# Row sums of adj by transpose and VectorE, first transfers in another order, a full tile for leftover taps, distances two groups at a time

## The chip, the core and the metric

One Trainium2 chip runs the program on one of its cores. A core has TensorE (PE; its weight loads are listed apart as PEld), VectorE (DVE), ScalarE (ACT), GpSimd (POOL) and SyncE (SP). Each engine works through its own queue in order; between engines there are semaphores. SP here only issues DMAs; ACT and POOL issue a few as well. The metric is the device time of one execution in microseconds, as a median of several runs, beside one execution taken by the profiler. Everything is float32.

## What is computed

Two graph layers over 128 graphs of 128 nodes with 256 features, `adj` sparse with about 3% of its entries set. Cut to what matters:

```python
# layer 0
in_degrees = jnp.sum(adj, axis=-1)
norm = jnp.power(in_degrees + 1e-06, -0.5)[..., None]
f_hom = jnp.einsum('bnd,de->bne', x, theta) * norm
f_hom = jnp.einsum('bnm,bmd->bnd', adj, f_hom) * norm
f_het = jnp.einsum('bnd,de->bne', x, W_h)
gate = sigmoid(x @ W_t + b_t)
x = layernorm(x + elu(gate * f_hom + (1 - gate) * f_het))
# layer 1
h = relu(bn1(conv1(xc)))            # xc: x with nodes along the last axis
h = bn2(conv2(h))                   # 17 taps along the nodes
x_conv = relu(h + xc)
s = x @ w_se.T + b_se               # three coordinates a node
dist = sq_n + sq_m - 2 s_n . s_m
A = jnp.exp(-dist) * adj
x_nmp = A @ relu(x @ w_msg.T + b_msg)
gi, gh = [x_conv, x_nmp] @ w_ih.T + b_ih, x @ w_hh.T + b_hh
x = layernorm(x + gru_update(gi, gh, x))
```

The degree of a node, the sum over a row of `adj`, scales both sides of layer 0's aggregation. The kernel receives `adj` turned, as `adjT[m, b, n]`, because a matmul's stationary operand is wanted with the summed axis on the partitions.

## The kernel before

The work has three stages.

**Layer 0 and the way into the convolution (0 to about 735 us).** A loop over rounds `t` from -1 to 63 (L511) takes two graphs a round (J = 2) and is pipelined by hand: in round t the projections of pair t (`l0_project`, L317 and L322) run beside the end of pair t-1 and the turning and first convolution of pair t-2. At the end of a round, `l0_turn(t+1)` (L291) transposes the next x by TensorE (L284), copies it from PSUM on VectorE (L288), and makes the degrees: for each graph one matmul with `adjT` stationary and a single column of ones streamed (L297). VectorE copies two columns out (L301), and POOL raises them to -1/2 (L161, L162; `inv_sqrt`). ScalarE uses the result as `norm` when it reads the next round's projection (L326). Then `l0_mix(t)` (L343) aggregates with `adjT` and VectorE reads that (L348).

In the same rounds TensorE also turns the taps of the 17-tap convolution into 136 frequency weights, written to memory as `w_d`. 32 units `w_unit` handle the first 128 frequencies from four row strips of 17 taps (L423). 19 units `v_unit` handle the 8 leftover ones (L455): two sets of seven input features by 17 taps, 119 rows, are multiplied by a block table `TL` of 56 columns. `TL` is filled by 14 small DMAs of POOL from the cosine table `T` (L247, in `way_back`, round 1). `units` and `units_v` put at most one such unit into a round. Taps come by `w_load` (L127, four DMAs each) into three tiles and by `v_load` (L447, two DMAs) into two rotating buffers. Before the loop SP issues `load(0)`, a weight, conv1's weights, `load(1)`, `w_load(0)` and `w_load(1)`; the other x and adjT follow from inside the rounds.

The order is written by hand for TensorE in all rounds, and for SP, VectorE and ScalarE from round 3 on (`manual_schedule`, L512). POOL's order, and that of the others in rounds -1 to 2, is found by the scheduler.

**The frequency products (735 to 912 us)** read `w_d`, multiply (L708, L721) and write `y_d`. The diff has nothing in them.

**Layer 1 (912 us to the end).** A loop over 32 groups of four graphs (G = 4; L1019), with only TensorE's order by hand. For a group: `l1_own` takes, on VectorE, a group's rows out of a turned table of coordinates (`turned`, made anew for every fourth group by two transposes, L860); `l1_kernel` makes the four distance tables by matmuls on 32-row strips (L880) into `acc`, a PSUM buffer of four banks of which there is one, which `l1_synth` (L808, L815, once in two groups) uses too; ScalarE takes the exponential (L884) and VectorE multiplies with adj (L887) into `AT`. `l1_gather` (L897) aggregates the messages with `AT`. `l1_gru` makes seven products a half group (`product`, L964), and calls `l1_kernel` of the next group between them, ahead of the fifth product of the second half.

Of the kernel before, what the change touches and what calls it, by code (L numbers as in the profile page):

```python
# [14 lines left out]
P = 128  # L15
# [19 lines left out]
def gnn_layers_kernel(ctx: ExitStack, tc: tile.TileContext, a: dict, out: bass.AP):  # L35
# [52 lines left out]
    SL = const.tile([P, P], F32, tag="SL", name="SL")  # L88
    T = taps.tile([P, M], F32, tag="T", name="T")
    FS = P // TAPS  # L90
    TL = taps.tile([P, ML * FS], F32, tag="TL", name="TL")
    conv1_w = acon.tile([P, NC, D + CO], F32, tag="conv1_w", name="conv1_w")
    shift1 = acon.tile([P, D], F32, tag="shift1", name="shift1")
    NW = 3
    wt = [taps.tile([P, 2, D], F32, tag=f"wt{i}", name=f"wt{i}") for i in range(NW)]


# [15 lines left out]
    def load(p):  # L113
        s = st[p] = {}
        s["x"] = io.tile([P, J, D], F32, tag="x", name=f"x_{p}")
        nc.sync.dma_start(s["x"], x[p * J : (p + 1) * J].rearrange("b n d -> n b d"))
        s["adjT"] = io.tile([P, J, P], F32, tag="adjT", name=f"adjT_{p}")
        nc.sync.dma_start(s["adjT"], adjT[:, p * J : (p + 1) * J, :])
# [27 lines left out]
    for i, q in enumerate("vmgb"):  # L146
        for k in range(2):
# [2 lines left out]
                vec[r : r + NC], a[f"L1_gnn_bn{k + 1}_{q}"].rearrange("(c p) -> c p", p=P)  # L150
            )

    nc.sync.dma_start(conv1_w[:, :, 0:D], a["conv1_wT"].rearrange("(c p) e -> p c e", p=P))
    nc.sync.dma_start(conv1_w[:, :, D:], a["w_seT"].rearrange("(c p) e -> p c e", p=P))
    load(1)
    w_load(0)
    w_load(1)

    def inv_sqrt(dst, src, eps, width):

# [74 lines left out]
    def way_back():  # L235

        AL = setup.tile([P, P // ML, ML], F32, tag="AL", name="AL")
        nc.vector.tensor_copy(AL, A[:, P:M].unsqueeze(1).to_broadcast([P, P // ML, ML]))
        nc.vector.memset(TL, 0.0)
        back = setup.tile([P, 1], F32, tag="back", name="back")  # L240
        nc.vector.memset(back, 2.0 / L)
        nc.vector.memset(back[0:2], 1.0 / L)

        cols = TL.rearrange("p (r i k) -> p r i k", r=2, i=FS)
        for i in range(FS):
            for r in range(2):
                nc.gpsimd.dma_start(  # L247
                    cols[i * TAPS : (i + 1) * TAPS, r, i, :], T[0:TAPS, P + r : M : 2]
                )
        tS = bank("S_ps")  # L250
        nc.tensor.transpose(tS[:, 0:P], A[:, 0:P], ident)
        nc.tensor.transpose(tS[:, P : 2 * P], AL.rearrange("p a b -> p (a b)"), ident)
        nc.vector.tensor_scalar(S, tS[:, 0:P], back, None, ALU.mult)
        nc.vector.tensor_scalar(SL, tS[:, P : 2 * P], 2.0 / L, None, ALU.mult)
# [21 lines left out]
    def nodes(q):  # L276
        return slice(q * P, (q + 1) * P)
# [13 lines left out]
    def l0_turn(p):  # L291
        s = st[p]
        s["xT"] = wf.tile([P, NC, J * P], F32, tag="xT", name=f"xT_{p}")
        transposed(s["x"], s["xT"], f"xT_{p}")
        deg = bank(f"deg_{p}")
        for j in range(J):
            nc.tensor.matmul(  # L297
                deg[:, j : j + 1], lhsT=s["adjT"][:, j, :], rhs=ones[:, 0:1], start=True, stop=True
            )
        norm = s["norm"] = small.tile([P, J], F32, tag="norm", name=f"norm_{p}")  # L300
        nc.vector.tensor_copy(norm, deg[:, 0:J])  # L301
        inv_sqrt(norm, norm, DEG_EPS, J)


# [137 lines left out]
        return [(f, min(FS, D - f)) for f in range(2 * FS * v, min(2 * FS * (v + 1), D), FS)]  # L442

    def v_load(v):
        t = taps.tile([P, 2, D], F32, tag="vt", bufs=2, name=f"v_t_{v}")
        for i, (f, n) in enumerate(v_sets(v)):
            nc.sync.dma_start(  # L447
                t[0 : n * TAPS, i, :], a["conv2_wT"][f : f + n].rearrange("i t o -> (i t) o")
            )
        s_v[v] = t  # L450

    def v_unit(v):
        n, sets = v_sets(v)[-1][1] * TAPS, len(v_sets(v))
        pl = bank(f"wl_ps_{v}")
        nc.tensor.matmul(  # L455
            pl[0 : ML * FS, 0 : sets * D], lhsT=TL[0:n],
            rhs=s_v[v][0:n, 0:sets].rearrange("p i o -> p (i o)"), start=True, stop=True,
        )
        ol = s_v[v] = taps.tile([ML * FS, 2, D], F32, tag="wl", name=f"wl_o_{v}")
        nc.vector.tensor_copy(  # L460
            ol[:, 0:sets].rearrange("p i o -> p (i o)"), pl[0 : ML * FS, 0 : sets * D]
        )
# [48 lines left out]
    for t in range(-1, NP):  # L511
        with tc.manual_schedule(engines={E.PE, E.SP, E.DVE, E.Activation} if t > 2 else {E.PE}):  # L512

            def on(q, work):
                if 0 <= q < NP:
                    work(q)

            def between():
                on(t - 1, l0_gate)
                on(t - 3, l1_analyse)  # L520

            def beside():
                on(t - 1, l0_elu)

            on(t - 2, l1_turn)
            l0_project(t, between, beside) if t >= 0 else between()
            on(t - 1, l0_norm)
            if t == 0:
                norms = batch_norms()
                next(norms)  # L530
                table(A, node, "A")
                table(T, lag, "T")

                cos, sin = T[:, 2:M:2], T[:, 3:M:2]
                both = setup.tile([P, M // 2 - 1], F32, tag="both", name="both")
                nc.vector.tensor_sub(both, sin, cos)
                nc.vector.scalar_tensor_tensor(sin, sin, -1.0, cos, ALU.mult, ALU.subtract)
                nc.vector.tensor_copy(cos, both)
            on(t - 2, l1_front)
            on(t - 2, l1_store)  # L540
            if t + 2 < NP:
                if 2 <= t + 2:
                    load(t + 2)
            else:
                m_load(t + 2 - NP)
            if t - 1 in units:
                w_store(units[t - 1])
            if t - 1 in units_v:
                v_store(units_v[t - 1])
            on(t + 1, l0_turn)  # L550
            if t == 2:
                v_load(0)
            if t == 3:
                nc.scalar.dma_start(w_msg, a["w_msgT"].rearrange("(c p) e -> p c e", p=P))
                nc.scalar.dma_start(b_msg, a["L1_gnn_b_msg"].partition_broadcast(P))
            if t == 1:
                next(norms, None)
                way_back()
                sctx.close()
                hpool = hstack.enter_context(tc.tile_pool(name="hpool", bufs=1))  # L560
                H = hpool.tile([P, NC, M, NB], F32, tag="H", name="H")
            on(t, l0_mix)
            if t in units_v:
                if units_v[t] + 1 < NV:
                    v_load(units_v[t] + 1)
                v_unit(units_v[t])
            if t in units:
                if units[t] + 2 < NU:
                    w_load(units[t] + 2)
                if t + 1 < NP:  # L570
                    w_unit(units[t])
# [299 lines left out]
        )  # L871
        st[g].update(turned=turned, own=own)

    def l1_kernel(g):
        s = st[g]
        turned, own = s["turned"], s["own"]
        pd = acc.tile([P, G, 512], F32, tag="acc", name=f"dist_ps_{g}")
        for q in range(G):
            k = slice(q * P // G, (q + 1) * P // G)
            nc.tensor.matmul(  # L880
                pd[:, q, 0:P], lhsT=turned[k, 0, :], rhs=own[k, :], start=True, stop=True
            )
        AT = ck.tile([P, G * P], F32, tag="AT", name=f"AT_{g}")
        nc.scalar.activation(  # L884
            AT.rearrange("p (q n) -> p q n", q=G), pd[:, :, 0:P], AF.Exp, scale=-1.0
        )
        nc.vector.tensor_mul(AT, AT, s["adjT"].rearrange("p q n -> p (q n)"))  # L887
        s["AT"] = AT


    def l1_gather(g):
# [115 lines left out]
    with tc.manual_schedule(engines={mybir.EngineType.PE}):  # L1007
        load_c(0)
        load_c(1)
        load_y(0)  # L1010
        for g in range(2):
            load_x1(g)
            l1_own(g)
        l1_project(0)
        l1_kernel(0)
        l1_project(1)
        l1_factors()
        l1_synth(0)
        for g in range(NG):  # L1019
            d = g // 2  # L1020
            if g + 2 < NG:
                load_c(g + 2)
                if g % 2 == 0:
                    load_y(d + 1)
                load_x1(g + 2)
            l1_gather(g)
            if 2 <= g + 1 < NG:
                l1_own(g + 1)
                l1_project(g + 1)
            l1_gru(g, 0)  # L1030
            if g % 2 == 1 and d + 1 < ND:
                l1_synth(d + 1)
            if g + 1 < NG:
                l1_gru(g, 1, {4: lambda: l1_kernel(g + 1)})
    with tc.manual_schedule(engines={E.PE, E.DVE, E.Activation}):
        l1_gru(NG - 1, 1)
    cctx.close()
# [41 lines left out]
```

## Time and profile before

| what | value |
|---|---|
| median of three runs | 2053.21 us (2051.23 to 2053.49) |
| the profiled execution | 2053.39 us, of which 2051.60 us from the first to the last instruction |
| granted TensorE clock, mean | 0.995 |
| DMA, read and written | 136.33 MB and 104.86 MB |

By stage, busy microseconds of each engine in the profiled execution:

| stretch, us | PE | DVE | ACT | POOL | granted clock | DMA share |
|---|---|---|---|---|---|---|
| 0 to 20.9 | 16.46 | 14.48 | 4.03 | 8.77 | 1.00 | 0.47 |
| 20.9 to 34.8 | 5.46 | 4.82 | 2.57 | 13.57 | 0.74 | 0.71 |
| 34.8 to 41.1 | 6.28 | 3.70 | 1.71 | 0.18 | 0.50 | 0.44 |
| 41.1 to 712 | 670.90 | 505.85 | 392.75 | 108.31 | 1.00 | 0.45 |
| 712 to 735 | 21.64 | 14.77 | 13.51 | 1.77 | 1.00 | 0.53 |
| 735 to 912 | 175.82 | 86.80 | 26.46 | 95.66 | 1.00 | 0.94 |
| 912 to 2051 | 1127.32 | 801.72 | 305.35 | 423.75 | 1.00 | 0.22 |

An engine's share of a stretch tells how full it is, not whether it sets the end; for that one looks at what each wait ended on. A float32 matmul is two records in this profile, a transpose is one; [...]the distance from one start to the next tells what one costs.

### The profile page before, as it was taken

To read this page: it belongs to the slowest core of one execution; us is meant where nothing else is said; L and a number is where in the kernel's file an instruction comes from. 1 tells how busy PE (TensorE), PEld (TensorE's weight loads), DVE (VectorE), ACT (ScalarE), POOL (GpSimd) and SP (SyncE) were. 2 spreads that over 40 slices of the span, in tenths; PEclk is the share of its full clock that TensorE was granted. 3 is DMA by queue.
4 is the path that set the end of the run, shared out by engine and by line. 5 is a ranking of instruction groups with operands and counts; after the bars stand their busy time and mean duration, and the time that the engine had idled before them with its cause. 6 is when DMAs were issued, how large, how long until landed. Compare 5 with 4: busy or idle time off the path is not lost.

```text
span 2051.6 us, 27050 instructions
## 1 busy us (share of the span) xinstructions
PE 2023.9 (99%) x8807; PEld 1384.2 (67%) x8807; DVE 1432.1 (70%) x2882; ACT 746.4 (36%) x1488; POOL 652.0 (32%) x869
## 2 busy tenths in 40 slices
PE   7999999999999999999999999999999999999997
PEld 4666766766766788886666666666666666666664
DVE  5777777777777764456767677676667767776766
ACT  2555655655555621112222222222322222232222
POOL 4111111111111135553433334333424333342431
PEclk8999999999999999999999999999999999999999
DMA  4544444444444479994222122222212222121100
GB/s 96 170 153 149 142 154 150 141 156 152 141 153 146 133 269 359 313 306 147 72 74 79 52 66 81 63 66 64 79 61 70 73 67 63 58 79 52 42 26 21
DMA packets 198044, 243.04 MB, mean 118 GB/s; under 512 B 16768, under 2 KB 141456, under 8 KB 197904
## 3 DMA queue, kind: packets, MB, share of 16 engines
q1 hardware_dynamic: 190880, 235.47, 35.3%
q10 hardware_dynamic: 6352, 5.78, 0.9%
q0 software_dynamic: 672, 0.06, 0.4%
q8 instruction: 71, 1.16, 0.3%
q14 instruction: 69, 0.57, 0.1%
HBM read 136.33 MB, written 104.86 MB: 118 GB/s over the span
## 4 chain that ended last, share of the span: by engine, by line
PE 96%; DVE 2%; POOL 1%; DMA 1%; ACT 0%; issue 0%; POOLq 0%; DVEq 0%; ACTq 0%; SPq 0%
PE g_ps L964 42%; PE f_ps L317 11%; PE conv_ps L387 5%; PE gate_ps L322 5%; PE msg_ps L844 5%; PE y_ps L708 5%; PE mix_ps L343 3%; PE coef_ps L407 3%; PE nmp_ps L897 3%; PE conv_ps L808 3%; PE z_ps L721 3%; PE x1T_ps L284 2%; PE w_ps L423 2%; PE xT_ps L284 1%; PE deg L297 1%; PE wl_ps L455 1%
## 5 line engine op out<-in xcount | busy, mean ns | idle before, releaser
L317 PE MATMUL f_ps<-w,xT 128*128 128x512 f32 x512 | 244.4, 600 | 0.1
L923 ACT ACTIVATE o<-o 128x1024 f32<-128x1024 f32 (+1 forms) x65 | 67.8, 1044 | 326.8 <-DVE o L1000 269.7
L161 POOL TENSOR_SCALAR rstd_b<-mv_b 128x2 f32<-128x2 f32 (+1 forms) x65 | 18.2, 280 | 529.6 <-DVE mv_b L262 529.6
L964 PE MATMUL g_ps<-t_h,sh 128*128 128x384 f32 x384 | 158.4, 494 | 0.0
L964 PE MATMUL g_ps<-t_c,sc 128*128 128x384 f32 x384 | 155.2, 486 | 0.0
L964 PE MATMUL g_ps<-t_m,sm 128*128 128x384 f32 x384 | 155.2, 486 | 0.0
L161 POOL TENSOR_SCALAR rstd_a<-mv_a 128x2 f32<-128x2 f32 x64 | 12.3, 193 | 436.4 <-DVE mv_a L262 380.1
L322 PEld LDWEIGHTS gate_ps<-w,xT 128*128 128x128 f32 x512 | 98.3, 192 | 69.1 <-issue 61.8
L322 PE MATMUL gate_ps<-w,xT 128*128 128x256 f32 x512 | 132.6, 382 | 0.0
L997 POOL TENSOR_TENSOR u<-u,p 128x512 f32<-128x512 f32 x63 | 79.8, 1267 | 163.3 <-DVE p L981 163.3
L317 PEld LDWEIGHTS f_ps<-w,xT 128*128 128x128 f32 x512 | 89.0, 193 | 62.9 <-issue 62.3
L708 PE MATMUL y_ps<-wb,H 128*128 128x256 f32 x544 | 128.5, 379 | 0.9 <-ACT H L411 0.8
L326 ACT ACTIVATE hom<-f_ps,norm 128x256 f32<-128x256 f32 x128 | 60.7, 474 | 187.6 <-PE f_ps L317 182.3
L271 ACT ACTIVATE y<-y,nb_b,rstd_b 128x256 f32<-128x256 f32 x128 | 70.0, 593 | 157.8 <-DVE nb_b L269 157.8
L387 PE MATMUL conv_ps<-conv_w,x1T 128*128 128x259 f32 x512 | 122.5, 381 | 0.0
L716 POOL TENSOR_TENSOR ws<-wb 128x512 f32<-128x512 f32 x67 | 93.2, 1390 | 88.8 <-PE z_ps L721 53.5
L708 PEld LDWEIGHTS y_ps<-wb,H 128*128 128x128 f32 x544 | 103.2, 190 | 15.4 <-issue 1.4
L844 PE MATMUL msg_ps<-w_msg,cx1T 128*128 128x256 f32 x480 | 108.7, 379 | 0.0
L964 PEld LDWEIGHTS g_ps<-t_c,sc 128*128 128x128 f32 x384 | 73.0, 190 | 50.9
L964 PEld LDWEIGHTS g_ps<-t_m,sm 128*128 128x128 f32 x384 | 73.0, 190 | 50.9 <-DVE sm L912 0.2
L387 PEld LDWEIGHTS conv_ps<-conv_w,x1T 128*128 128x128 f32 x512 | 97.1, 190 | 14.7 <-ACT w_o L427 0.2
L964 PE MATMUL g_ps<-w_hhT_w,cx1T 128*128 128x384 f32 x256 | 105.0, 492 | 0.0
(228 smaller groups left out, 4524.8 us busy)
## 6 DMA issues: line engine op xcount, KB each, us to landing
wb<-w_d SPq DMA_DIRECT2D x68, 512.0 KB
w_d<-w_o SPq DMA_DIRECT2D x256, 128.0 KB
y_d<-yb SPq DMA_DIRECT2D x68, 256.0 KB
x<-in_x SPq DMA_DIRECT2D x64, 256.0 KB
cx1T<-x1T_d SPq DMA_DIRECT2D x64, 256.0 KB
yt<-y_d SPq DMA_DIRECT2D x32, 512.0 KB
cx<-x_d SPq DMA_DIRECT2D x32, 512.0 KB
x_d<-x SPq DMA_DIRECT2D x63, 256.0 KB
```

The costliest lines, as they stand in the source:

```text
L271: nc.scalar.activation(dst[:, q, :], src[:, q, :], AF.Identity, bias=nb[:, q : q + 1], scale=rstd[:, q : q + 1],)
L284: nc.tensor.transpose(t[:, (c * J + j) * P : (c * J + j + 1) * P], src[:, j, c * P : (c + 1) * P], ident,)
L317: nc.tensor.matmul(pf, lhsT=xT[:, c, nodes(j)], rhs=w0[:, c, 0 : 2 * D], start=(c == 0), stop=(c == NC - 1),)
L322: nc.tensor.matmul(pg[:, j * D : (j + 1) * D], lhsT=xT[:, c, nodes(j)], rhs=w0[:, c, 2 * D : 3 * D], start=(c == 0), stop=(c == NC - 1),)
L343: nc.tensor.matmul(pm[:, j * D : (j + 1) * D], lhsT=adjT_[:, j, :], rhs=hom[:, j, :], start=True, stop=True,)
L387: nc.tensor.matmul(ph[:, 0 : D + CO], lhsT=s["x1T"][:, c, nodes(j)], rhs=conv1_w[:, c, :], start=(c == 0), stop=(c == NC - 1),)
L708: nc.tensor.matmul(py[:, blk, :], lhsT=coefs(blk if k == 0 else 2 * k + 1 - blk, c), rhs=w[:, c, blk, :], start=(c == 0), stop=(c == NC - 1),)
L716: nc.gpsimd.tensor_tensor(ws, w[:, :, 0, :], w[:, :, 1, :], ALU.add)
L844: nc.tensor.matmul(pm[:, j * D : (j + 1) * D], lhsT=x1T[:, c, nodes(q)], rhs=w_msg[:, c, :], start=(c == 0), stop=(c == NC - 1),)
L923: nc.scalar.activation(rz, rz, AF.Tanh, scale=0.5)
L964: nc.tensor.matmul(pg[:, lo : lo + 3 * P], lhsT=s[f"f{kind}"][i][:, pr, :], rhs=factors[kind][i], start=(k == 0), stop=(k == 2), skip_grou ...
L997: nc.gpsimd.tensor_tensor(u4, u2, p5, add)
```

## The change

Four edits.

1. *Degrees.* `l0_turn` transposes both adjT blocks back into PSUM, and VectorE sums over the free axis into `norm`. The matmuls with a column of ones and the copy of two columns are gone.
2. *Transfers of the first rounds.* `load(1)` goes ahead of conv1's weights; `w_load(0)` and `w_load(1)` move from before the loop into rounds 0 and 1, behind that round's `load`; `v_load(0)` and `v_load(1)` go to rounds 2 and 3. From then on `v_load` runs two units ahead and is issued behind the unit whose buffer it fills.
3. *Full tile for leftover taps.* `TL` becomes 128 columns wide, the tap tiles are two fixed ones whose last rows are set to zero once, and the matmul uses all 128 rows and columns. The copy out still takes 56 partitions.
4. *Distances by twos.* `l1_kernel` takes one or two groups: eight matmuls on strips in a row, then for each group the exponential and the product. It is called in odd groups only. `l1_own` of group g+2 moves to the top of group g; `AT` gets a third buffer.

```diff
-    TL = taps.tile([P, ML * FS], F32, tag="TL", name="TL")
+    TL = taps.tile([P, P], F32, tag="TL", name="TL")
+    vt = [taps.tile([P, 2, D], F32, tag=f"vt{i}", name=f"vt{i}") for i in range(2)]
...
+    load(1)
     nc.sync.dma_start(conv1_w[:, :, 0:D], a["conv1_wT"].rearrange("(c p) e -> p c e", p=P))
     nc.sync.dma_start(conv1_w[:, :, D:], a["w_seT"].rearrange("(c p) e -> p c e", p=P))
-    load(1)
-    w_load(0)
-    w_load(1)
...
+        for t in vt:
+            nc.vector.memset(t[96:], 0.0)
...
-        cols = TL.rearrange("p (r i k) -> p r i k", r=2, i=FS)
+        cols = TL[:, 0 : ML * FS].rearrange("p (r i k) -> p r i k", r=2, i=FS)
...
-        deg = bank(f"deg_{p}")
+        adj = bank(f"adj_ps_{p}")
         for j in range(J):
-            nc.tensor.matmul(
-                deg[:, j : j + 1], lhsT=s["adjT"][:, j, :], rhs=ones[:, 0:1], start=True, stop=True
-            )
+            nc.tensor.transpose(adj[:, nodes(j)], s["adjT"][:, j, :], ident)
         norm = s["norm"] = small.tile([P, J], F32, tag="norm", name=f"norm_{p}")
-        nc.vector.tensor_copy(norm, deg[:, 0:J])
+        nc.vector.reduce_sum(
+            norm, adj[:, 0 : J * P].rearrange("p (j n) -> p j n", j=J), axis=mybir.AxisListType.X
+        )
         inv_sqrt(norm, norm, DEG_EPS, J)
...
     def v_unit(v):
-        n, sets = v_sets(v)[-1][1] * TAPS, len(v_sets(v))
+        sets = len(v_sets(v))
         pl = bank(f"wl_ps_{v}")
         nc.tensor.matmul(
-            pl[0 : ML * FS, 0 : sets * D], lhsT=TL[0:n],
-            rhs=s_v[v][0:n, 0:sets].rearrange("p i o -> p (i o)"), start=True, stop=True,
+            pl[:, 0 : sets * D], lhsT=TL, rhs=vt[v % 2][:, 0:sets].rearrange("p i o -> p (i o)"),
+            start=True, stop=True,
         )
...
                 if 2 <= t + 2:
                     load(t + 2)
+                if 0 <= t < 2:
+                    w_load(t)
+                if 2 <= t < 4:
+                    v_load(t - 2)
...
-            if t == 2:
-                v_load(0)
...
             if t in units_v:
-                if units_v[t] + 1 < NV:
-                    v_load(units_v[t] + 1)
                 v_unit(units_v[t])
+                if units_v[t] + 2 < NV:
+                    v_load(units_v[t] + 2)
...
+    def l1_kernel(*groups):
+
+        pd = acc.tile([P, G, 512], F32, tag="acc", name=f"dist_ps_{groups[0]}")
+        for i, g in enumerate(groups):
+            turned, own = st[g]["turned"], st[g]["own"]
+            for q in range(G):
+                k = slice(q * P // G, (q + 1) * P // G)
+                nc.tensor.matmul(
+                    pd[:, q, i * P : (i + 1) * P], lhsT=turned[k, 0, :], rhs=own[k, :],
+                    start=True, stop=True, skip_group_check=True,
+                )
+        for i, g in enumerate(groups):
+            AT = st[g]["AT"] = ck.tile([P, G * P], F32, tag="AT", bufs=3, name=f"AT_{g}")
+            nc.scalar.activation(
+                AT.rearrange("p (q n) -> p q n", q=G), pd[:, :, i * P : (i + 1) * P],
+                AF.Exp, scale=-1.0,
             )
...
+            nc.vector.tensor_mul(AT, AT, st[g]["adjT"].rearrange("p q n -> p (q n)"))
...
-        l1_kernel(0)
+        l1_kernel(0, 1)
...
                 load_x1(g + 2)
+                l1_own(g + 2)
             l1_gather(g)
             if 2 <= g + 1 < NG:
-                l1_own(g + 1)
                 l1_project(g + 1)
             l1_gru(g, 0)
...
-                l1_gru(g, 1, {4: lambda: l1_kernel(g + 1)})
+
+                l1_gru(g, 1, {4: lambda: l1_kernel(g + 1, g + 2)} if g % 2 == 1 else {})
```

More of the change, by code (lines that the diff above doesn't have):

```diff
@@ L444, in v_load @@
     def v_load(v):
-        t = taps.tile([P, 2, D], F32, tag="vt", bufs=2, name=f"v_t_{v}")
+        t = vt[v % 2]
         for i, (f, n) in enumerate(v_sets(v)):
@@ L449, in v_load @@
             )
-        s_v[v] = t
     def v_unit(v):
-        n, sets = v_sets(v)[-1][1] * TAPS, len(v_sets(v))
+        sets = len(v_sets(v))
         pl = bank(f"wl_ps_{v}")
         nc.tensor.matmul(
-            pl[0 : ML * FS, 0 : sets * D], lhsT=TL[0:n],
-            rhs=s_v[v][0:n, 0:sets].rearrange("p i o -> p (i o)"), start=True, stop=True,
+            pl[:, 0 : sets * D], lhsT=TL, rhs=vt[v % 2][:, 0:sets].rearrange("p i o -> p (i o)"),
+            start=True, stop=True,
         )
@@ L872, in l1_own @@
         st[g].update(turned=turned, own=own)
[L874 to L881, printed above, removed]
-            )
[L883 to L888, printed above, removed]
+    def l1_kernel(*groups):
[13 more added lines that the diff above has]
+                AF.Exp, scale=-1.0,
+            )
+            nc.vector.tensor_mul(AT, AT, st[g]["adjT"].rearrange("p q n -> p (q n)"))
     def l1_gather(g):
```

## The prediction

> **What bounds the kernel now.** I read the page first: the engines' busy shares and the chain of waits.
>
> ```profile
> PE 2023.9 (99%) x8807; PEld 1384.2 (67%) x8807; DVE 1432.1 (70%) x2882; ACT 746.4 (36%) x1488; POOL 652.0 (32%) x869
> ...
> PE 96%; DVE 2%; POOL 1%; DMA 1%; ACT 0%; issue 0%; POOLq 0%; DVEq 0%; ACTq 0%; SPq 0%
> ```
>
> TensorE is on 96% of the chain that ended last. A busy PE need not be a PE at its peak, so I read its timeline too. There, each row starts where the row before stops streaming; what counts is start to start. The groups' idle columns give PE 9.3 us before xT_ps, 4.0 before x1T_ps and under 3 elsewhere, nearly all in the first 35 us; a table by stage has it busy for 670.9 of the 670.9 us from 41 to 712. (From 735 to 912 us the DMA engines are 94% busy, with PE still at 175.8 of 177; the change touches nothing there.) So in the long stretches a matmul removed is time removed, as long as nobody else then comes late.
>
> A layer-0 round without extra units, and one with a unit of leftover taps (PE timeline: start, length, line, tiles, count):
>
> ```profile
> 222.59 0.60 PE L284 MATMUL xT_ps<-ident,x 128*128 128x128 f32 x4
> 223.02 0.50 PE L297 MATMUL deg<-ones,adjT 128*128 128x1 f32 x4
> 223.39 1.11 PE L343 MATMUL mix_ps<-hom,adjT 128*128 128x256 f32 x4
> 224.33 0.60 PE L284 MATMUL x1T_ps<-ident,x 128*128 128x128 f32 x4
> ...
> 200.97 1.11 PE L343 MATMUL mix_ps<-hom,adjT 128*128 128x256 f32 x4
> 202.01 1.06 PE L455 MATMUL wl_ps<-v_t,TL 119*56 119x512 f32 x2
> 203.00 0.66 PE L284 MATMUL x1T_ps<-ident,x 128*128 128x128 f32 x4
> ```
>
> **Degrees.** Each of the two degree matmuls of a round is two records, and though one column is streamed, each waits for its weights: four records take 223.02 to 223.39, 0.37 us, and the next row also starts badly: mix takes 0.94 us (223.39 to 224.33), while four records of the same width take 0.86 us in gate_ps (205.22 to 206.08). A transpose of a 128x128 block is one record: four take 0.43 us (222.59 to 223.02), 0.108 each. After the change the stretch from 223.02 to 224.33, 1.31 us, becomes 2 x 0.108 + 0.86 = 1.08 us: 0.23 us less in every round. Rounds turned before 41 us lie in the start, treated below; 61 are left: **14.0 us**.
>
> On VectorE a 150 ns copy (L301, 128x2) becomes a sum over 128x256 in PSUM. No row shows that operation. Bounds: not below the copy's 0.15 us, as it reads more; not above the 128x512 PSUM copy's 0.69 us, which reads twice as much. Nearest is BATCH_NORM_STATS2 (reads 256 elements a partition, writes 6): 0.41 us. I take 0.41, so 0.26 us more. Where it lands (VectorE timeline):
>
> ```profile
> 211.97 0.69 DVE L288 COPY xT<-xT_ps 128x512 f32<-128x512 f32 x1
> 212.58 0.15 DVE L301 COPY norm<-deg 128x2 f32<-128x2 f32 x1
> 213.29 0.88 DVE L348 SCALAR_TENSOR_TENSOR hom<-mix_ps,norm,het 128x256 f32<-128x256 f32 x2 [0.56 <-PE mix_ps L343]
> 214.95 0.69 DVE L288 COPY x1T<-x1T_ps 128x512 f32<-128x512 f32 x1 [0.78 <-PE x1T_ps L284]
> ```
>
> Behind it VectorE idles 0.56 us until mix is done. Mix will come 0.23 us sooner, leaving 0.33 us of cover for 0.26 us. Were the sum 0.69 us, the overflow of 0.2 us meets the 0.78 us idle before the x1T copy. The Trainium skill, "VectorE: DVE Perf Modes", Rules for kernel authors, speaks against this edit: tensor_reduce runs at 1x, "the slowest DVE op", to be kept off the hot path. Its table (errata section; PSUM source, 120 cycles plus one per element at 0.96 GHz) gives an estimate of (120 + 256) / 0.96 = 392 ns, near the row. On the path, 64 times 0.24 us more would be 15 us and cancel the edit; by the trace's idle it costs **0**.
>
> Who is late next? In plain rounds, over all rounds of the stretch, x (ACT L271) is ready at least 0.96 us before its transpose, the xT copy 0.86 us before f_ps, and POOL's norm 1.66 us before ACT uses it. Less 0.23 us (norm: less 0.26 more) all stay above 0.6 us. VectorE's 83.1 us per 110 us (75%) becomes about 80%. Nothing takes over.
>
> **Leftover taps.** From mix to f_ps a unit's round takes 203.50 - 200.97 = 2.53 us, a plain one 224.77 - 223.39 = 1.38: the unit costs 1.15 us, of which streaming two 512-wide records is 0.86 (f_ps: four in 1.72). The rest is at the edges: mix before it is 0.10 longer, wl_ps itself 0.99, x1T behind it 0.06 longer. It is an edge of tile shape: w_ps (17 rows) and dist_ps (32 rows) show the same steps, 0.09 us extra on each side, and rows of 128*128 beside one another never do. A full tile should pay none: 0.285 x 18, and about as much for the half-wide last unit: **5.4 us**. Bounds: 0 if the edges are not of shape, 5.5 if all goes. The skill, "TensorE: Matmul & The Clock Gate", LDWEIGHTS section, says weight loading lasts (columns)/1.2 ns whatever the rows, and its back-to-back formula counts moving columns alone. By these the edit gains nothing, and loading 128 columns in place of 56 is 60 ns more, 38 times, an estimate of 2.3 us lost if bare. The trace: 128 ns for the 56-column load, 190 ns for full ones, and full ones hide behind f_ps without a gap. I follow the trace.
>
> v_load(v+2) now stands on SP behind a wait for this round's wl_ps. Queued behind it are w_load (none in these rounds) and the next round's x1 store, which waits for ACT later anyway: 0. The data come two units ahead instead of one. Zeroing the tap tiles and wider TL: two or three memsets in VectorE's idle first 2 us; 0.
>
> **Distances by twos** (PE timeline, layer 1):
>
> ```profile
> 947.64 0.81 PE L964 MATMUL g_ps<-t_m,sm 128*128 128x384 f32 x2
> 948.38 0.50 PE L880 MATMUL dist_ps<-own,turned 32*128 32x128 f32 x8
> 948.81 0.91 PE L964 MATMUL g_ps<-t_h,sh 128*128 128x384 f32 x2
> 949.56 0.81 PE L964 MATMUL g_ps<-t_c,sc 128*128 128x384 f32 x2
> ```
>
> 947.64 to 949.56 is 1.92 us; two pairs of 128x384 undisturbed take 1.29. A visit costs 0.63 us, mostly for changing shape twice and filling. Its eight records run as two waves of four. A second group adds two waves. Their price: 0.11 us each if weights load behind streaming (nmp_ps: 16 such records in 1.78 us), 0.21 if not (the start-to-start of the two waves here, whose first contains the fill). I take 0.11, since the loads of the second wave start 0.11 us after the first's. 32 visits of 0.63 become 16 of 0.85: **6.5 us** (3.2 at 0.21). Cover: AT lies ready 3.6 us before nmp_ps; a second exponential (0.60) and product (0.68) do not use that up. adjT is fetched more than a group ahead into three buffers. l1_own moves to the top of a group: the turn matmuls keep their cost; own (0.27 us) lands in a VectorE that is 70% busy. 0.
>
> **The start.** Here the views are the waits of PE and POOL's timeline:
>
> ```profile
> 25.86 1.09 PE L284 MATMUL xT_ps<-ident,x 128*128 128x128 f32 x4 [4.97 <-DMA x<-in_x]
> ...
> 34.80 1.40 PE L284 MATMUL x1T_ps<-ident,x 128*128 128x128 f32 x4 [3.48 <-ACT x L271]
> ```
>
> ```profile
> 16.52 1.28 POOL L247 DMA_DIRECT2D TL<-T  x1 [0.65 <-DVE norm L301]
> ...
> 20.22 12.63 POOL L247 DMA_DIRECT2D TL<-T  x12
> 32.93 0.19 POOL L161 TENSOR_SCALAR rstd_a<-mv_a 128x2 f32<-128x2 f32 x1
> ```
>
> load(2) is queued on SP behind the eight w_load issues (8.59 to 15.67 us). With them behind it, x_2 is issued about 7 us sooner and the 4.97 us wait goes. But the chain doesn't run through that: x1T_0 needs x_0 normalised, this needs rstd_a, and POOL issues 14 small TL transfers from 16.5 to 32.9 us first. They hang on T, not on any reordered transfer. So PE will just wait at x1T_0 instead, some 8 us or more: **0**, less 0.3 us lost since a degree sum (0.26 longer) stands on VectorE before T's last copy. Taps loaded later are needed only at 47 us.
>
> **Sum.** 14.0 + 5.4 + 6.5 - 0.3 = 25.6 us. The profiled execution took 2053.39 us (span 2051.60), giving 2027.8; from the median of 2053.21 it is 2027.6.
>
> **Rivals.**
> 1. POOL's order of the first rounds is not fixed by hand. If rstd_a slips in among the TL issues, x1T_0 comes as soon as mv_a allows: its second half waited behind the late xT_2 copy, and without it is ready near 24.5; rstd, nb and x take 2 to 3 us: x1T_0 at about 27.5, 7.3 sooner: 2020. If the clock also stays up (0.50 granted from 34.8 to 41.1, some 3 us lost), 2017. For: mv_a comes earlier. Against: rstd_a stands earlier in the program and was still put behind all fourteen.
> 2. Shape edges stay: waves cost 0.21 and tap edges remain in half: 3.3 + 2.7 less: 2034.
> 3. Slower: in layer 1 VectorE's order is the scheduler's. conv2_ps and dist_ps share the one acc buffer; the last xcT is read out only 0.83 us before the distances begin, in each of 15 odd groups. If moved own and doubled AT products push that read back, PE waits; it decides at 0.83 + 25.6/15 = 2.5 us, four operations of 0.68. With five (3.4 us) it is 15 x 2.57 = 39 us: 2066. Against: no stall today, and the additions come behind the read.
>
> **Chances.** Forecast 0.62, rival 1 0.22, rival 2 0.11, rival 3 (with smaller forms that end near the old time) 0.05. Forecast's own uncertainty is about 3 us; the range for 8 in 10 goes from rival 1 to rival 2: 2018 to 2035. A change under 0.2% (4 us) can't be told from none: faster 0.94, same 0.02, slower 0.04.
>
> **What would show it.** Right: adj transposes with 0.11 us spacing, mix at 0.86; wl_ps 0.86 without longer neighbours; 16 visits of 16 records at about 0.85; no wait for x_2, but a longer one at x1T_0. Wrong: PE idle before f_ps or x1T in plain rounds (the sum is on the path), before dist_ps (rival 3), or x1T_0 before 30 us (rival 1).

## The result, and the profile after

| | before | after |
|---|---|---|
| median of the runs compared | 2052.56 us (2051.23 to 2053.49, 4 runs) | 2026.76 us (2025.63 to 2027.40, 4 runs) |
| ratio to before, 95% interval | | 0.9874 [0.9857, 0.9891] |
| the profiled execution, its span | 2053.39 us, 2051.60 us | 2027.40 us, 2025.62 us |
| granted TensorE clock, mean | 0.995 | 0.995 |

The change saves 25.8 us by the medians and 26.0 us by the spans. Where it lies can be read from the PE timelines of both kernels, by the start of the same matmul in each (for g_ps of its last record, for the others of the row):

| mark | before, us | after, us | difference | of it since the mark above |
|---|---|---|---|---|
| first x1T_ps | 34.80 | 33.70 | -1.10 | -1.10 |
| fourth xT_ps | 45.45 | 44.04 | -1.41 | -0.31 |
| last xT_ps | 705.50 | 685.14 | -20.36 | -18.95 |
| last f_ps | 711.92 | 691.04 | -20.88 | -0.52 |
| first turn_ps of layer 1 | 912.56 | 893.07 | -19.49 | +1.39 |
| last g_ps | 2039.31 | 2013.32 | -25.99 | -6.50 |

So there are two gains, 19.5 us in the rounds of layer 0 and 6.5 us in layer 1. The small steps at both ends of layer 0 are looked at further down.

The page's busy shares, and its chain of waits:

```profile
PE 1993.2 (98%) x8679; PEld 1372.1 (68%) x8679; DVE 1461.8 (72%) x2884; ACT 746.2 (37%) x1488; POOL 645.5 (32%) x869
...
PE 96%; DVE 1%; POOL 1%; DMA 0%; ACT 0%; issue 0%; SPq 0%; POOLq 0%; DVEq 0%; ACTq 0%
```

PE has lost 30.7 us of busy time, VectorE has gained 29.7 us (about 17 of them by the sums, as 64 records of 0.41 us stand for copies of 0.15; the rest lies mostly in layer 1), and PE still carries 96% of the chain. There are 128 PE records fewer, two for each of 64 rounds: four one-column records have become two transposes.

A round with a unit of leftover taps, in the PE timeline of after (start, length, line, tiles, count):

```profile
130.56 0.27 PE L286 MATMUL xT_ps<-ident,x 128*128 128x128 f32 x1
130.67 0.38 PE L299 MATMUL adj_ps<-ident,adjT 128*128 128x128 f32 x2
130.89 1.03 PE L345 MATMUL mix_ps<-hom,adjT 128*128 128x256 f32 x4
131.76 1.02 PE L456 MATMUL wl_ps<-vt,TL 128*128 128x512 f32 x2
132.62 0.60 PE L286 MATMUL x1T_ps<-ident,x 128*128 128x128 f32 x4
133.05 1.02 PE L319 MATMUL f_ps<-w,xT 128*128 128x512 f32 x2
```

The two transposes take 0.22 us (130.67 to 130.89), mix takes 0.87 (to 131.76), wl_ps 0.86 (to 132.62), and x1T behind it 0.43 like any other. None of these rows has an edge any more. From one xT_ps to the next, a plain round went from 10.03 to 9.80 us, a round with a main unit from 11.25 to 11.02, and one with a leftover unit from 11.17 to 10.66.

What VectorE does in the meantime, in its timeline of after:

```profile
55.70 0.69 DVE L290 COPY xT<-xT_ps 128x512 f32<-128x512 f32 x1
56.30 0.42 DVE L301 TENSOR_REDUCE norm<-adj_ps 128x2 f32<-128x256 f32 x1
56.78 0.88 DVE L350 SCALAR_TENSOR_TENSOR hom<-mix_ps,norm,het 128x256 f32<-128x256 f32 x2
58.44 0.69 DVE L290 COPY x1T<-x1T_ps 128x512 f32<-128x512 f32 x1 [0.78 <-PE x1T_ps L286]
```

The sum takes 0.39 to 0.42 us over all 64 rounds. The idle time of 0.56 us that stood ahead of hom is used up. The round shown has a main unit, and in such rounds the 0.78 us before the x1T copy are there as before; in a plain round the copy follows hom without a gap, after as before.

Distances in layer 1, PE timeline of after:

```profile
962.09 0.81 PE L970 MATMUL g_ps<-t_m,sm 128*128 128x384 f32 x2
962.83 0.73 PE L884 MATMUL dist_ps<-own,turned 32*128 32x128 f32 x16
963.49 0.91 PE L970 MATMUL g_ps<-t_h,sh 128*128 128x384 f32 x2
964.24 0.81 PE L970 MATMUL g_ps<-t_c,sc 128*128 128x384 f32 x2
```

From 962.09 to 964.24 it is 2.15 us; less 1.29 for two undisturbed pairs, a visit of sixteen records costs 0.86. Its second wave of four starts 0.21 us behind the first, as before the change; the third and the fourth, which the second group adds, follow by 0.11 us each.

### The profile page after: what moved, and what is told of

It is laid out like the page before. It is cut to its first block, busy times and chain, and to the rows that moved or that the text cites. A ratio compares the mean times of both kernels' runs of the same rounds, so it can differ in the third digit from the quotient of the medians.

```text
span 2025.6 us, 26703 instructions
## 1 busy us (share of the span) xinstructions
PE 1993.2 (98%) x8679; PEld 1372.1 (68%) x8679; DVE 1461.8 (72%) x2884; ACT 746.2 (37%) x1488; POOL 645.5 (32%) x869
## 4 chain that ended last, share of the span: by engine, by line
PE 96%; DVE 1%; POOL 1%; DMA 0%; ACT 0%; issue 0%; SPq 0%; POOLq 0%; DVEq 0%; ACTq 0%
PE g_ps L970 42%; PE f_ps L319 11%; PE y_ps L711 6%; PE gate_ps L324 5%; PE conv_ps L389 5%; PE msg_ps L847 5%; PE coef_ps L409 3%; PE nmp_ps L903 3%; PE conv_ps L811 3%; PE z_ps L724 3%; PE mix_ps L345 3%; PE w_ps L425 2%; PE x1T_ps L286 2%; PE xT_ps L286 1%; PE conv_ps L818 1%; PE wl_ps L456 1%
## 5 line engine op out<-in xcount | busy, mean ns | idle before, releaser
L160 POOL TENSOR_SCALAR rstd_b<-mv_b 128x2 f32<-128x2 f32 (+1 forms) x65 | 12.5, 192 | 529.9 <-DVE mv_b L264 529.9
```

## The experiments

All kernels differ from the changed one only by the edit shown, and each was timed beside the kernel before. "Span" compares its profiled execution with the 2025.62 us above. Steps are differences between marks of the table above, against the changed kernel.

How far such a step wanders by itself must be known first. Over the profiles of the five kernels that have the same work at the start (the changed one, the two with other taps, and those with distances of one and of four groups), the fourth xT_ps starts between 43.76 and 45.11 us. The stage from the last f_ps to layer 1, which no edit touches, is shorter than in the changed kernel's profile in eleven of twelve experiments, by 0.1 to 1.9 us, and 0.5 us longer in one. So single steps of one microsecond at these two places say nothing. Where no edit touches them, the rounds repeat within 0.2 us, and so does layer 1 but for one profile (56 columns), which is 0.6 us longer at a single row of conv_ps.

### Degrees: the old way back

```diff
-            nc.tensor.transpose(adj[:, nodes(j)], s["adjT"][:, j, :], ident)
+            nc.tensor.matmul(
+                adj[:, j : j + 1], lhsT=s["adjT"][:, j, :], rhs=ones[:, 0:1], start=True, stop=True
+            )
...
-        nc.vector.reduce_sum(
-            norm, adj[:, 0 : J * P].rearrange("p (j n) -> p j n", j=J), axis=mybir.AxisListType.X
-        )
+        nc.vector.tensor_copy(norm, adj[:, 0:J])
```

> The changed kernel (2026.8 us), with the degrees again by two matmuls with one column of ones and a copy of two columns. Theory (TensorE sets every layer-0 round, each term adds): a round from xT to xT becomes 0.23 us longer, 61 times 0.23 = 14.0 us, so 2040.8; periods 11.25, 10.89 and 10.03 us in place of 11.02, 10.66 and 9.80. Rival (part of the gain came from elsewhere, or VectorE's sum cost something that now comes back): under 10 us, 2036 or less.

Measured: 2041.58 us, ratio to before 0.9948 [0.9935, 0.9962]; span +13.2 us, of which the rounds are +13.72 and the last one +0.23. Its PE timeline has both costs again, 0.36 us for the four one-column records and 1.04 for the mix row (0.96 in the changed kernel, where a main unit follows too):

```profile
231.07 0.50 PE L299 MATMUL adj_ps<-ones,adjT 128*128 128x1 f32 x4
231.43 1.11 PE L345 MATMUL mix_ps<-hom,adjT 128*128 128x256 f32 x4
232.47 1.14 PE L425 MATMUL w_ps<-wt,T 17*128 17x512 f32 x8
```

The degrees are worth the 14 us of the sum.

### Degrees: turned by an ordinary matmul

```diff
-            nc.tensor.transpose(adj[:, nodes(j)], s["adjT"][:, j, :], ident)
+            nc.tensor.matmul(
+                adj[:, nodes(j)], lhsT=s["adjT"][:, j, :], rhs=ident, start=True, stop=True
+            )
```

> The changed kernel, with adjT turned by ordinary matmuls against the identity instead of transposes; the sum on VectorE stays. Theory (a transpose is one record, an ordinary float32 matmul two, at 0.11 us each): 4 x 0.112 in place of 2 x 0.109, 0.23 us a round, 61 rounds, +14.0: 2040.8, the whole gain of the edit. Rival (the gain comes from leaving out one-column matmuls and their bad follower mix, not from the transpose): about +0 to +3, 2027 to 2030.

Measured: 2040.62 us, ratio 0.9940 [0.9927, 0.9952]; span +13.5 us, rounds +13.72 again. Its PE timeline shows why:

```profile
220.73 0.61 PE L299 MATMUL adj_ps<-ident,adjT 128*128 128x128 f32 x4
221.17 1.03 PE L347 MATMUL mix_ps<-hom,adjT 128*128 128x256 f32 x4
222.04 0.60 PE L286 MATMUL x1T_ps<-ident,x 128*128 128x128 f32 x4
```

Four records in 0.44 us in place of two in 0.22. Mix has no edge (0.87 us), so here the loss is the second record alone, 0.22 us a round. Moving the sum to VectorE this way brings nothing, since the four records and mix (0.44 + 0.87 us) take as long as the one-column records and the longer mix of the old way (0.37 + 0.94); the gain is that a transpose is a single record.

### The sum made twice

```diff
+        nc.vector.reduce_sum(
+            norm, adj[:, 0 : J * P].rearrange("p (j n) -> p j n", j=J), axis=mybir.AxisListType.X
+        )
```

> The changed kernel, with VectorE's sum over the rows made twice in every round (same result, 0.41 us more on VectorE). Theory (the sum lies under VectorE's wait for mix and the 0.3 to 0.8 us idle before the x1T copy): +0 to 1 us, 2027 to 2028. Rival (a sum on VectorE is on the path, so that the first one costs too): 61 x 0.41 = +25 us, 2052. Between: only plain rounds, 12 of them, lack the cover: 12 x 0.3 = +4, 2031.

Measured: 2028.42 us, ratio 0.9883 [0.9869, 0.9896]; rounds -0.00 us. The steps that make the span 0.8 us longer are at the start (+2.19, and -1.52 in the stage before layer 1), where POOL began its fourteen issues 0.85 us later and the two norm operations moved in with rstd_a. VectorE's timeline:

```profile
210.79 0.69 DVE L290 COPY x1T<-x1T_ps 128x512 f32<-128x512 f32 x1 [0.48 <-PE x1T_ps L286]
...
219.67 0.41 DVE L301 TENSOR_REDUCE norm<-adj_ps 128x2 f32<-128x256 f32 x1
220.12 0.42 DVE L304 TENSOR_REDUCE norm<-adj_ps 128x2 f32<-128x256 f32 x1
220.46 0.87 DVE L353 SCALAR_TENSOR_TENSOR hom<-mix_ps,norm,het 128x256 f32<-128x256 f32 x2
221.24 0.68 DVE L290 COPY x1T<-x1T_ps 128x512 f32<-128x512 f32 x1
```

The first row is from a round with a main unit: there 0.48 of the 0.78 us ahead of the x1T copy are left. The others are from a plain round, where the copy has no gap ahead of it in the changed kernel either; it starts 2.81 us behind the start of xT_ps on PE, in place of 2.52, and still PE loses nothing in the rounds. The cover is more than twice what the edit needs; where it ends was not tried.

### Leftover taps: rows and columns apart

128 rows and 56 columns:

```diff
-            pl[:, 0 : sets * D], lhsT=TL, rhs=vt[v % 2][:, 0:sets].rearrange("p i o -> p (i o)"),
+            pl[0 : ML * FS, 0 : sets * D], lhsT=TL[:, 0 : ML * FS],
+            rhs=vt[v % 2][:, 0:sets].rearrange("p i o -> p (i o)"),
```

> The changed kernel, with the leftover-tap matmul on all 128 rows but only 56 stationary columns. Theory (the edges are paid for a change of the array's shape, and 56 columns are the change): the whole 0.285 us a unit comes back, +5.4, 2032.2, with wl_ps 0.31 behind mix and 0.52 before x1T. Rival (119 of 128 rows were the change): +0, 2026.8.

119 rows and 128 columns:

```diff
-            pl[:, 0 : sets * D], lhsT=TL, rhs=vt[v % 2][:, 0:sets].rearrange("p i o -> p (i o)"),
+            pl[:, 0 : sets * D], lhsT=TL[0 : FS * TAPS],
+            rhs=vt[v % 2][0 : FS * TAPS, 0:sets].rearrange("p i o -> p (i o)"),
```

> The changed kernel, with the leftover-tap matmul on 119 rows and all 128 columns. Theory (columns are what changed the shape; 119 rows still take all four row strips): +0, 2026.8, units as in the changed kernel. Rival (rows): +5.4, 2032.2.

Measured: with 56 columns 2032.77 us, ratio 0.9900 [0.9883, 0.9916], rounds and last round +5.57 us; with 119 rows 2027.35 us, ratio 0.9879 [0.9864, 0.9893], rounds +0.12. The PE timeline, first with 56 columns, then with 119 rows:

```profile
131.45 1.03 PE L345 MATMUL mix_ps<-hom,adjT 128*128 128x256 f32 x4
132.41 1.07 PE L456 MATMUL wl_ps<-vt,TL 128*56 128x512 f32 x2
133.40 0.66 PE L286 MATMUL x1T_ps<-ident,x 128*128 128x128 f32 x4
133.90 1.88 PE L319 MATMUL f_ps<-w,xT 128*128 128x512 f32 x4
```

```profile
131.98 1.03 PE L345 MATMUL mix_ps<-hom,adjT 128*128 128x256 f32 x4
132.84 1.02 PE L456 MATMUL wl_ps<-vt,TL 119*128 119x512 f32 x2
133.71 0.49 PE L286 MATMUL x1T_ps<-ident,x 128*128 128x128 f32 x3
```

With 56 columns mix takes 0.96, wl_ps 0.99 and x1T 0.50 us: all three edges are back. With 119 rows they are 0.86, 0.87 and no edge. What counts here is the width of the stationary tile; the zeroed last rows are not needed for the time.

### Distances one group at a time

```diff
-        l1_kernel(0, 1)
+        l1_kernel(0)
...
-                l1_gru(g, 1, {4: lambda: l1_kernel(g + 1, g + 2)} if g % 2 == 1 else {})
+                l1_gru(g, 1, {4: lambda: l1_kernel(g + 1)})
```

> The changed kernel, with the distances of one group at a time again, 32 visits (own still made at the top of a group, AT with three buffers). Theory (a visit costs 0.63 us, the second group's two waves 0.11 each): 16 x (0.63 - 0.22) = +6.5, 2033.3. Rival (waves cost 0.21 each, the rest of what layer 1 gained came from moving own or from VectorE's order): +3.2, 2030.0.

Measured: 2033.47 us, ratio 0.9907 [0.9894, 0.9921]; layer 1 +6.52 us. The moved l1_own and the third buffer stay in this kernel, so all of the 6.5 us come from the doubled visits.

### Transfers of the first rounds in the old order

Those of `v_load` stay as changed.

```diff
-    load(1)
     nc.sync.dma_start(conv1_w[:, :, 0:D], a["conv1_wT"].rearrange("(c p) e -> p c e", p=P))
     nc.sync.dma_start(conv1_w[:, :, D:], a["w_seT"].rearrange("(c p) e -> p c e", p=P))
+    load(1)
+    w_load(0)
+    w_load(1)
...
-                if 0 <= t < 2:
-                    w_load(t)
```

> The changed kernel, with the first transfers in the old order: conv1's weights ahead of load(1), both w_load before the loop. Theory (POOL's fourteen TL issues set x1T_0, so the wait for x_2 is hidden): x_2 is waited for some 5 us near 21 us, x1T_0 starts within 0.5 us of the changed kernel's 33.7, and the time is 2026.8 plus 0 to 0.5. Rival (the reordered transfers made the start shorter): +5, 2032.

Measured: 2026.92 us, ratio 0.9868 [0.9854, 0.9883]; the first x1T_ps +0.97, the fourth xT_ps 0.26 us earlier than in the changed kernel, as only 3.2 us of the work between them run at a granted clock of 0.50, in place of 5.7. By itself the new order is worth nothing. PE's timeline:

```profile
26.20 1.09 PE L288 MATMUL xT_ps<-ident,x 128*128 128x128 f32 x4 [5.25 <-DMA x<-in_x]
...
34.67 1.39 PE L288 MATMUL x1T_ps<-ident,x 128*128 128x128 f32 x4 [3.30 <-ACT x L275]
```

PE waits for x_2 again (5.25 us), and the wait at the first x1T_ps is 3.30 us in place of 11.09: whichever wait comes first, POOL's issues set when the second ends.

### The table's transfers on SP instead of POOL

```diff
-                nc.gpsimd.dma_start(
+                nc.sync.dma_start(
                     cols[i * TAPS : (i + 1) * TAPS, r, i, :], T[0:TAPS, P + r : M : 2]
```

> The changed kernel, with the fourteen TL transfers issued by SP instead of POOL. Theory (POOL's issues hold back rstd_a): rstd_a follows mv_a at 23.7, x1T_0 starts 1.9 later at about 25.6 instead of 33.7: -8.1, and up to 3 more if TensorE's clock doesn't fall in the shorter gap: 2015.7 to 2018.7. Rival (the start is bound by something else than POOL's queue, such as the landing of other transfers): under 2 us, 2025 or more.

Measured: 2028.57 us, ratio 0.9879 [0.9864, 0.9894], no faster than the change. The start did what the theory said, and then the gain went back. PE's timeline:

```profile
26.13 0.33 PE L286 MATMUL x1T_ps<-ident,x 128*128 128x128 f32 x1 [2.54 <-ACT x L273]
...
37.23 1.14 PE L425 MATMUL w_ps<-wt,T 17*128 17x512 f32 x8
46.84 1.39 PE L286 MATMUL x1T_ps<-ident,x 128*128 128x128 f32 x4 [8.47 <-ACT x L273]
```

The first x1T_ps comes 7.6 us sooner, and the second waits for ScalarE's x_1. What holds that up, from the table of waits (who waits, for whom, us in total, times, longest), and then SP's timeline:

```profile
ACT x L273 <- DMA x_d<-x: 9.2, 1, 9.2
```

```profile
29.14 13.14 SPq L249 DMA_DIRECT2D TL<-T  x14
42.38 0.46 SPq L117 DMA_DIRECT2D x<-in_x  x1
42.94 0.40 SPq L401 DMA_DIRECT2D x_d<-x  x1
```

SP issues the fourteen transfers in a row, 0.94 us each, and x_0's store stands behind them until 42.94 us. By the table, x_1 is only written when that store has read the buffer. The wait left POOL's queue and came up in SP's. It costs more than its 8.47 us: behind it the granted clock is 0.50 until 51.64 us, for 4.8 us of work, an estimate of 2.4 us more. Together that is 10.9 of the 11.0 us that the rounds take longer.

### The same, with the transfers in the old order

Both edits above together.

> TL transfers issued by SP, and the first transfers in the old order. Theory (with POOL free the late x_2 shows: xT_2's copy stands before the second half of mv_a on VectorE): mv_a at 27.8, x1T_0 at about 29.7, so 4 us later than with both: about 2021 to 2023. So the reordered transfers are worth about 4 us here and nothing with TL on POOL. Rival (their order never matters): the same as with TL on SP and the new order.

Measured: 2027.15 us, ratio 0.9874 [0.9859, 0.9889]. With POOL free the order of the transfers shows: the first x1T_ps starts at 28.66 us, 2.5 later than in the kernel before this one, because PE waits 3.53 us for x_2, until 24.45. At the fourth xT_ps only 0.5 us of that are left (36.09 against 35.62), as the granted clock from 27 to 34 us is 0.95 here and 0.76 there. Then the same wait for the store follows.

### The table in seven transfers

POOL keeps them, but one moves both halves of the table; VectorE first copies the table with its halves apart.

```diff
+                TE = setup.tile([P, 2, ML // 2], F32, tag="TE", name="TE")
+                nc.vector.tensor_copy(TE, T[:, P:M].rearrange("p (k r) -> p r k", r=2))
...
-            for r in range(2):
-                nc.gpsimd.dma_start(
-                    cols[i * TAPS : (i + 1) * TAPS, r, i, :], T[0:TAPS, P + r : M : 2]
-                )
+            nc.gpsimd.dma_start(cols[i * TAPS : (i + 1) * TAPS, :, i, :], TE[0:TAPS])
```

> The table goes to the 119 rows of cols in 7 transfers of 17x2x4 elements in place of 14 of 17x4, still issued by POOL behind norm_1; VectorE first copies the table with its two halves apart. Theory: each issue costs POOL some 1.05 us whatever it moves and rstd_a_0 waits for all of them, so 7 x 1.05 = 7.4 us from about 17 us: rstd_a at about 24.4 us in place of 31.8, x1T_0 at about 26.2 in place of 33.7, xT_3 about 8 us earlier, and since SP's queue is not lengthened nothing is given back: 2018 to 2019 us. Rival 1: the issue time goes by what is moved, 7 x 2.1 us, so rstd_a stays at 31.8 and the time at 2026.8. Rival 2: the first rounds run into SP's queue all the same (x_0's store stands behind the load of adjT_4, which SP is through with at some 32.7 us), x1T_1 waits, and 2022 to 2026 us is what is left.

Measured: **2019.51 us** (2018.61 to 2020.46, five runs), ratio 0.9841 [0.9828, 0.9854]. Its interval lies wholly below the changed kernel's: 32.7 us less than before, where the change has 25.8. POOL's timeline:

```profile
17.88 6.95 POOL L248 DMA_DIRECT2D TL<-TE  x7 [0.42 <-DVE diag L227]
24.91 0.18 POOL L160 TENSOR_SCALAR rstd_a<-mv_a 128x2 f32<-128x2 f32 x1
```

Seven issues take 0.99 us each though each moves twice as much, so rstd_a stands at 24.91 us. With the table on SP, where it waited for mv_a alone, it stood at 24.27; little more is to be had there. PE's timeline has the first x1T_ps:

```profile
26.78 1.39 PE L283 MATMUL x1T_ps<-ident,x 128*128 128x128 f32 x4 [3.62 <-ACT x L270]
```

It starts 6.9 us sooner, the fourth xT_ps 8.0 us sooner, and from there the rounds take as long as in the changed kernel (0.00). x_0's store goes out at 30.58 us, so nothing is given back.

### Distances of four groups at a time

The diff is cut further: `l1_own` of four groups is called together, in every fourth group.

```diff
-        own = ck.tile([P, P], F32, tag="own", name=f"own_{g}")
+        own = ck.tile([P, P], F32, tag="own", bufs=4, name=f"own_{g}")
...
-            AT = st[g]["AT"] = ck.tile([P, G * P], F32, tag="AT", bufs=3, name=f"AT_{g}")
+            AT = ats[g] = ck.tile([P, G * P], F32, tag="AT", bufs=5, name=f"AT_{g}")
...
+    def l1_masked(g):
+        AT = st[g]["AT"] = ats.pop(g)
+        nc.vector.tensor_mul(AT, AT, st[g]["adjT"].rearrange("p q n -> p (q n)"))
...
+                def ahead():
+                    if g % 4 == 3:
+                        l1_kernel(g + 1, g + 2, g + 3, g + 4)
+                    l1_masked(g + 1)
+                l1_gru(g, 1, {4: ahead})
```

> The changed kernel, with distances of four groups at a time (exponentials of all four at once, each product with adj one group ahead). Theory: 8 visits of 0.63 + 6 x 0.11 = 1.29 in place of 16 of 0.85: 13.6 - 10.3 = -3.3, 2023.5. Rival (VectorE and ScalarE, not ordered by hand here, come late with AT or with reading conv2_ps out of the shared buffer): 2027 or more, with TensorE waiting before nmp_ps or dist_ps.

Measured: 2032.52 us, ratio 0.9908 [0.9892, 0.9925]; layer 1 +3.47 us. The visits became cheaper as the theory said: eight of 1.30 us, 10.4 in all where the change has 13.7. New waits cost more than that. PE's timeline at the first of them, and the table of waits around it:

```profile
918.75 0.91 PE L974 MATMUL g_ps<-t_m,sm 128*128 128x384 f32 x2 [3.54 <-DVE sm L922]
```

```profile
DVE AT L899 <- DMA cadjT<-in_adjT: 5.6, 2, 4.5
...
PE g_ps L974 <- DVE sm L922: 3.5, 1, 3.5
```

VectorE stood at a product with adj whose load had not come, and sm, which PE waits for, stood behind it. From start to start that is 3.7 us, once. Some 1.7 us more are small delays in later groups. These 5.4 us are most of the 6.8 that went (3.3 + 3.5); the rest isn't traced to a row.

### Four at a time, and the table on SP

Both edits together.

> Distances by fours and TL transfers issued by SP, to see whether both gains add. Theory: they lie at the two ends of the program, so -3.3 and -8 to -11 add: 2012 to 2016. Rival (the earlier end of layer 0 is given back where DMAs are 94% busy): 2018 or more.

Measured: 2032.26 us, ratio 0.9904 [0.9889, 0.9919]: a miss. The first x1T_ps came 7.39 us sooner and 10.63 were given back; layer 1 took 3.86 us more. The two losses simply add.

## Why the prediction was right

- **Degrees.** Put at 0.23 us a round; plain rounds are 0.23 shorter, and putting the old way back costs 13.95 us where 14.0 stood in the sum. Both parts of it are seen in the rows: the records go from 0.37 to 0.22 us, and mix from 0.94 to 0.87.
- **The sum on VectorE at nothing.** Taken at 0.41 us by the nearest row, it measures 0.39 to 0.42. That the idle time hides it holds even for two. The reserve of 0.78 us behind it was read in a round with a main unit and isn't there in plain rounds; it was not needed. The advice of the Trainium skill ("VectorE: DVE Perf Modes", Rules for kernel authors) to consider restructuring when this operation is on the hot path took nothing from the gain, since VectorE's path here isn't the one that sets the end; the estimate of 392 ns from the page's cycle table agrees with the trace.
- **Leftover taps.** 19 units of 0.285 us were 5.4; the narrow tile back costs 5.6. The prediction spoke of an edge of shape and left open which side; it is the columns. The loss of 2.3 us that was estimated from the skill's rule for weight loads ("TensorE: Matmul & The Clock Gate", LDWEIGHTS), had the longer loads lain bare, did not come: with the wider tile wl_ps takes 0.86 us, no more than its two records stream.
- **Distances.** 6.5 predicted, 6.50 between the marks, 6.52 by the experiment. Of the two prices for an added wave, 0.11 was right.
- **Who is late next.** Nobody: PE is busy for 648.9 of the 648.9 us from 41.1 to 690 us. The slower rival would have shown as a wait of PE ahead of dist_ps; the start-to-start there has only the edge of shape, 0.09 us.
- **The start.** Said to be worth nothing because POOL's fourteen issues decide, with a longer wait at the first x1T_ps. That wait is there, 11.09 us, and none for x_2:

```profile
33.70 1.40 PE L286 MATMUL x1T_ps<-ident,x 128*128 128x128 f32 x4 [11.09 <-ACT x L273]
```

```profile
16.20 0.69 POOL L161 TENSOR_TENSOR norm<-norm,neg_half 128x2 f32<-128x2 f32 x1
16.85 14.90 POOL L249 DMA_DIRECT2D TL<-T  x14
31.83 0.19 POOL L160 TENSOR_SCALAR rstd_a<-mv_a 128x2 f32<-128x2 f32 x1
```

  The term of this step was off in size and sign: a loss of 0.3 us was predicted, 1.4 us were gained by the fourth xT_ps, 1.1 of them at the first x1T_ps. POOL's order, which nobody writes by hand, now has norm_1 ahead of all issues, so they take 14.90 us without a break, where before it stood among them and they took 16.3; with the old degrees put back it stands among them again. The other 0.3 us are the granted clock: from the first x1T_ps to the fourth xT_ps it takes 10.65 us before and 10.34 after, of which 6.31 and 5.69 us were at 0.50; with that half taken off, both come to 7.5 us. But the first x1T_ps wanders by as much over the five kernels with the same start (33.44 to 34.88 us), so a gain of this size is not shown.
- **What the sum left out.** 1.4 us were lost between the last f_ps and layer 1, where a wait of PE of 1.82 us is new (PE's timeline before, then after):

```profile
731.01 1.99 PE L486 MATMUL early_ps<-w_msg,mx1T 128*128 128x256 f32 x8
```

```profile
711.90 1.99 PE L487 MATMUL early_ps<-w_msg,mx1T 128*128 128x256 f32 x8 [1.82 <-DMA mx1T<-x1T_d]
```

  Before, the same matmul followed at once. In seven of the fourteen kernels profiled it starts 1.3 to 2.1 us later behind the last f_ps than in the quickest, in the other seven 0 to 0.5 us later, in a pattern that no edit explains: 0.4 us with 119 rows and 1.9 with 56 columns, which differ in nothing near it. SP issues the load 14.9 us behind the last f_ps in both of these, so it is not the issue that is late. Why the load lands late in some stays open. So the sum of 25.6 us against 25.8 measured is right by its large terms; that it comes so near is luck, since two small ones that it missed, 1.4 us gained and 1.4 lost, nearly cancel.
- **Rivals.** The first, an earlier rstd_a, didn't happen, but its price for the place held: it said 2020 us, and the seven transfers, which do bring rstd_a forward, gave 2019.5. The second and the third didn't happen either: the edges of the leftover taps are gone, an added wave costs 0.11 us, and PE doesn't wait in layer 1.

## What to carry to other kernels

Before a wait is moved, ask what ends next to last: here loads in another order brought nothing while POOL's issues held the same matmul, moving those issues to SP brought nothing because they held up a store that frees a buffer there, and only issuing fewer of them did. On an engine that is always busy, price the changes of tile shape and the second records too, and not only the columns that stream. Work may be put on a busy-looking engine if the idle time right behind it is longer than what is added; doubling it on purpose tells how much is left.

## What was not expected of the hardware

- The issue of a small DMA costs the engine that makes it about a microsecond, and it doesn't go by size here: on POOL 1.06 us for 17x4 elements (14 in 14.90) and 0.99 for 17x2x4 (7 in 6.95); on SP 0.94 (14 in 13.14).
- A stationary tile of 56 columns between tiles of 128 costs 0.29 us for a visit of two records; one of 119 rows costs nothing.
- The granted clock is 0.50 for a while around a long idle time of PE, and comes back to 1.00 only some microseconds after the work has. In the changed kernel PE idles for 11.09 us, to 33.70; the clock is 0.50 from 25.7 to 39.4 us, so 5.7 us of work run at half the clock, an estimate of 2.8 us lost. With the wait cut to 3.62 us, it is 0.50 from 26.9 to 30.3 us, for 3.4 us of work, an estimate of 1.7 lost. The 1.1 us between them made the 6.9 us at the first x1T_ps into 8.0 at the fourth xT_ps. The length of the wait alone doesn't decide it: in layer 1, with four groups at a time, the clock stayed at 1.00 around a wait of 3.54 us, and with the table on SP as well it was 0.50 for 3.4 us behind one of 2.73.
